# A Winograd-multiplied graph attention on one core: the last two block sums on VectorE, W_v's differences in another order, one counting pass later, attention paced anew

## The chip, the core and the metric

The kernel runs on one core of a Trainium2 chip. The metric is the device time of one execution in microseconds. The core's engines run side by side, each through its own list of instructions in order: TensorE (PE in the profile, PEld for its weight loads) multiplies, VectorE (DVE) and ScalarE (ACT) work on tiles in on-chip memory, GpSimd (POOL) does the same and also issues the gathers and scatters by index, and SyncE (SP) issues plain DMA transfers. An instruction waits at the head of its engine's list until the semaphores that it needs have come; what stands behind it on that engine waits too.

## The reference

```python
h = jnp.maximum(_layernorm(x, axis=-1), 0.0)
...
q = sent_embed @ W_q.T + b_q
k = sent_embed @ W_k.T + b_k
v = sent_embed @ W_v.T + b_v
scale = 1.0 / math.sqrt(sent_embed.shape[-1])
z = scale * (q @ k.T)
spare_z = z * adj_tensor
spare_z = jnp.where(spare_z == 0.0, jnp.asarray(-10000.0, spare_z.dtype), spare_z)
attn = jax.nn.softmax(spare_z, axis=1)
out = attn @ v
return jax.nn.relu(out)
...
x = x + _L0_gnn_ref(h, adj, ...)
```

x is 2708 x 1024, adj is 2708 x 2708 with about four ones in a row, the weights are 1024 x 1024, and everything is in float32. Since adj is so thin, the kernel never forms q @ k.T. It finds the edges of each row, gathers the few rows of h that they name, and takes scores and weighted sums of those alone.

## The kernel before

**Stages.** First the product of the two weights W_q and W_k is formed (called M, in four blocks; about the first 105 us), while the rows of x are normalised to h and written to `h_dram`, and while adj is searched. A tile is 128 rows. The search of tile k has two halves: `found` (steps f, i) takes the places of the ones with VectorE, and `counted` (step p) sums the row with one pass of ScalarE over the whole tile of adj (line 368). Both read the same buffer of three; whichever of them comes first in the program issues the load (`loaded`, line 360, on SP). Then rows are sorted by their number of edges, in two halves, and all later work goes by sorted tiles of 128 rows.

**Units.** The main loop (line 1225 on) runs over 20 units of two tiles each. Units 0 to 9 are q units: rows of h times M, which gives the q rows. Units 10 to 19 are o units: the attention's weighted sums u times W_v, which gives the output. Each unit is one Winograd product of a 2 x 2 block matrix: seven block products instead of eight. In the order of PE's list, for unit n, they are:

- second: s2·T1 into bank Y (line 1010, `psy<-wlow,s`)
- third: a12·M10 into bank X (`ps<-M,a`)
- fourth: s4·M11 into bank Z (`ps<-M,s`)
- fifth: s3·T2 into bank Y (`psy<-wlow,s`)
- then the first two of the next unit, `opened(n+1)`: a11·M00 into its X (`ps<-M,a`) and s1·T0 into its Z (`ps<-wlow,s`)
- seventh: a22·T3 into bank Y (`psy<-wlow,a`)

Each is four matmuls of 128x512 in float32, which the trace shows as eight records. T0 to T3 are four differences of the blocks of M, kept in `wlow`. When the q units are over, M's place takes the four blocks b11, b12, b21, b22 of W_v, loaded one by one during units 8 and 9 (line 1259), and VectorE forms T0 to T3 anew at line 1263: T0 = b12 - b11, T1 = b22 - T0, T2 = b22 - b12, T3 = b21 - T1. Each may be written only when unit 9 has used the old one.

**What surrounds the products.** `blocks` (line 711) prepares a unit's operands. The rows are either turned by PE (line 415, `pt<-ident,qr`, four groups of transposes in a unit) and copied by ScalarE (line 718), or, in units 10 to 14 (the "faced" tiles), loaded in quarters (line 700) and turned by VectorE (line 705). Then s1 and s3 are sums of two blocks on VectorE, and s2 and s4 are sums on the engine named in the call at line 1281, GpSimd for nearly all units (line 722, function `put`). `multiply` (line 1044) calls `after(0)` to `after(6)` between the products. The results leave the banks by ScalarE copies (line 1023: Y starts as a copy of X; line 1026: p5 from Z; line 1054: u2 from Y after the second product; lines 1088, 1099 in q units, 1118, 1134 in o units) and by two additions on VectorE: c12 (line 1094, or 1125 in o units) takes Z, c22 (line 1091, or 1121) takes Y after the fifth product. In o units ScalarE first copies Y for c22 (line 1075), in units 6 to 9 VectorE reads Y itself, and the seventh product, which goes on in Y, must wait for that reader.

**The attention** is a stream of steps on VectorE: `scores` (line 863, a product with a running sum over 128x1024), `weights` (small operations at lines 893 to 911 and, on ScalarE, line 872 or 898 and the start of the weighted sum at line 912 or 903) and `sums` (line 923). The gathered rows lie in 11 slots, 13 once M's place is free; a slot is filled by a gather on GpSimd (line 610) when its reader is done. Every call of `after` draws `share` microseconds of estimated steps from the stream (`advance`, line 999), so `share` fixes how many attention steps stand in VectorE's list between two steps of a unit. VectorE's list is in the order in which the program is written; the lists of PE, SP and, for the later units, of ScalarE and GpSimd are ordered by a scheduler that works with its own estimates.

**The steps table.** The search and the normalisation are written by hand into the units: `steps_at[(n, i)]` names what `follow` does in `after(i)` of unit n.

Of the kernel before, what the change touches and what calls it, by code (L numbers as in the profile page):

```python
# [65 lines left out]
def tile_preln_masked_attention(  # L66
# [12 lines left out]
    nc = tc.nc  # L79
# [353 lines left out]
    T = wlow.rearrange("p (k a) (b w) -> p k (a b) w", a=2, b=2)  # L433
# [180 lines left out]
    rows_of = {}  # L614
    FIRST = EARLY // 2
# [95 lines left out]
    def blocks(xa, xb, eng=None):  # L711


        ops = {}

        def held(name, bank):
            ops[name] = small(name).rearrange("p (c q) -> p c q", q=P)
            nc.scalar.copy(ops[name], bank)

        def put(name, a, b, op, eng=None):  # L720
            ops[name] = small(name).rearrange("p (c q) -> p c q", q=P)
            step = (eng or nc.vector).tensor_tensor(ops[name], a, b, op=op)  # L722
            if eng is None:
                behind.append(step)

        def faced_half(name, xt, s):
            ops[name] = small(name).rearrange("p (c q) -> p c q", q=P)
            faces(ops[name], xt, s * 4, s * 4 + 4)

        def upper():  # L730
            for s, name in enumerate(("a11", "a12")):
                if is_faced(xa):
                    faced_half(name, xa, s)
                else:
                    held(name, half_turned(xa, s))

        def lower():
            if is_faced(xb):
                faced_half("a22", xb, 1)
                faced_half("s3", xb, 0)  # L740
                put("s1", ops["a22"], ops["s3"], ALU.add)
                behind.append(nc.vector.tensor_sub(ops["s3"], ops["a11"], ops["s3"]))
            else:
                held("a22", half_turned(xb, 1))
                a21 = half_turned(xb, 0)
                put("s1", ops["a22"], a21, ALU.add)
                put("s3", ops["a11"], a21, ALU.subtract)
            put("s2", ops["s1"], ops["a11"], ALU.subtract, eng)
            put("s4", ops["a12"], ops["s2"], ALU.subtract, eng)

        return ops, upper, lower
# [11 lines left out]
    def natural_rows(n):  # L763
# [3 lines left out]
    ops_of = {0: blocks(*rows_of.pop(0))}  # L767
# [14 lines left out]
    steps_at = {(0, 0): "s4-5 p8 e9 +19 +20 +21", (0, 1): "r4 +0 +1 +2 i10.0-1", (0, 3): "p10", (0, 4): "i10.2-3 a4",  # L782
# [4 lines left out]
    steps_ahead = {(1, 5): "o1", (3, 6): "o0"}  # L787

# [199 lines left out]
    faced_tiles, whole_second = set(), []  # L988
# [236 lines left out]
    for n, unit in enumerate(units):  # L1225
        kind, ta, tb = unit
        now[:] = n, 0
        if n == FIRST:
            ordered.close()
            ordered.enter_context(tc.manual_schedule(engines={mybir.EngineType.DVE}))  # L1230
            nc.sync.dma_start(bp_dram, bp_sb[0:1, :])
        turn = n in (0, FIRST - 1)
        share = (20.0 if kind == "q" else 19.8) / 7
        nxt = units[n + 1] if n + 1 < len(units) else None
        if nxt is not None and nxt[0] == "o":
            share -= 1.3 / 7 * len(set(nxt[1:]) & faced_tiles)
        results = (q_results if kind == "q" else o_results)(ta, tb)

        def after(i):
            now[1] = i  # L1240
            if (n, i) in steps_ahead:
                follow(steps_ahead[n, i])
            if (n, i) == (2, 5):
                owe(8)
                owe(9)
                rows_of[FIRST] = load_rows(units[FIRST])
                owe(10)
                owe(6)
                owe(7)
                rows_of[FIRST + 1] = load_rows(units[FIRST + 1])  # L1250
                pooled.close()
            if (n, i) == (FIRST, 1):
                for g in slots[:HIGH - 3]:
                    nc.vector.memset(g, 0.0)
            b11, b12, b21, b22 = M[:, 0, 0], M[:, 0, 1], M[:, 1, 0], M[:, 1, 1]
            for at, place, src in (((-1, 0), b12, of_wv(0, 1)), ((0, 0), b11, of_wv(0, 0)), ((0, 2), T[:, 1], of_wv(1, 1)),
                                   ((0, 3), b21, of_wv(1, 0)), ((0, 4), b22, of_wv(1, 1))):
                if (n - last_q, i) == at:
                    nc.sync.dma_start(place, src)
            for at, place, a, b in (((0, 2), T[:, 0], b12, b11), ((0, 5), T[:, 1], T[:, 1], T[:, 0]),  # L1260
                                    ((1, 0), T[:, 3], b21, T[:, 1]), ((1, 1), T[:, 2], b22, b12)):
                if (n - last_q, i) == at:
                    nc.vector.tensor_sub(place, a, b)  # L1263
            if (n - last_q, i) == (1, 1):
                free.extend(M.rearrange("p i j (a c) w -> p i j a (c w)", a=2)[:, 0, 1, a, :] for a in range(2))
            if (n, i) == (FIRST, 5):
                next(stream)
            if (n, i) == (FIRST, 6):
                chain.append(behind[-1])
                next(stream)  # L1270
                nc.vector.tensor_tensor(bad, bad, total, op=ALU.not_equal)
            if (n, i) == (FIRST + 1, 6):
                marked(EARLY, NT)
            if (n, i) == (FIRST + 2, 4):
                nc.vector.tensor_scalar(msq, msq, MLIMIT, None, op0=ALU.is_gt)
            if n > FIRST + 1 or n == FIRST + 1 and i > 1:
                advance(share)
            if nxt is not None:

                if i == (3 if n == 0 else 4 if turn else 0):  # L1280
                    ops_of[n + 1] = blocks(*rows_of[n + 1], nc.gpsimd if n + 1 != FIRST - 1 else None)
                    with tc.issue_after(products[-1].ins) if n + 1 == FIRST else nullcontext():
                        ops_of[n + 1][1]()
                if i == (4 if n == 0 else 5 if turn else 2):
                    ops_of[n + 1][2]()
                    rows_of.pop(n + 1)
                    if n == last_q - 1:
                        all_rows()
                if i == 3:
                    banks_of[n + 1] = banks_for(bp_sb)  # L1290
                if i == 6 and n + 2 < FIRST:
                    natural_rows(n + 2)
                if i == (2 if n in (FIRST, last_q) else 4) and n + 2 > FIRST and n + 2 < len(units) and n + 2 not in rows_of:
                    while units[n + 2][0] == "o" and not done.issuperset(units[n + 2][1:]):
                        advance(1.0)
                    rows_of[n + 2] = load_rows(units[n + 2])
            if (n, i) in steps_at:
                follow(steps_at[n, i])
            if (n, i) == (3, 4):
                searched()  # L1300
            if (n, i) == (3, 5):
                for s in range(8, HIGH):
                    for c in range(0, D, D // 4):
                        clear = nc.gpsimd.memset(slots[s][:, c:c + D // 4], 0.0)
                        tc.add_manual_dep(clear.ins, counted_at[-1].ins.name,
                                          mybir.DependencyInfo(mybir.DependencyClass.Sync, mybir.DependencyReason.DATA),
                                          reason="not beside the counts")
            if i == 3 and units[n - 1][0] == "o" and NT - 2 in units[n - 1][1:]:
                tail(NT - 1)
            if nxt is None and i == 1:  # L1310
                while alone not in done:
                    advance(1.0)
                r, = load_rows(("o", alone))
                single["turned"] = turned(r, "alone")
            if nxt is None and i == 3:
                single["banks"] = banks_for(bp_sb)
            if n == last_q - 1 and i == 4:

                nc.sync.dma_start(bp_sb, bv.to_broadcast([P, D]))
            if (n, i) == (last_q, 1):  # L1320
                nc.vector.tensor_sub(bp_sb[:, NB:], bp_sb[:, NB:], bp_sb[:, :NB])

        multiply(n, results, after)
# [54 lines left out]
    with tc.If(some > 0):  # L1378
# [19 lines left out]
        with tc.tile_pool(name="big", bufs=1, side="right") as big, tc.tile_pool(  # L1398
# [34 lines left out]
            with tc.For_i(0, NT) as i:  # L1433
# [9 lines left out]
                q = gen.tile([P, D + 1], FT, tag="q", name="g_q")  # L1443
# [111 lines left out]
```

## Time and profile before

| | |
|---|---|
| median of 3 runs | 646.67 us (646.43 to 647.45) |
| the profiled execution | 648.94 us |
| its span, first to last instruction | 647.2 us |
| mean granted TensorE clock | 0.995 |
| DMA | 176.97 MB, 273 GB/s over the span |

The span is 1.7 us shorter than the profiled execution's own time; the rest lies before the first and behind the last instruction. In a row of the profile, `out<-in` are the program's tile names without numbers, the figure behind the engine's name is the line of the kernel, and a bracket at the end of a timeline's row says how long the engine sat idle just before it and what ended that. The timeline's first two columns are the start and the length in microseconds, and equal rows that follow each other are merged (their count stands behind the x). Rows with PEq, SPq or ACTq are the sequencer of that engine, as it issues a transfer.

### The profile page before, as it was taken

The page shows a single profiled execution, that of the slowest core. Times are in us where ns is not written, and L with a number is a line of the kernel's source. Part 1 is how long each engine was busy: PE and PEld are TensorE (multiplying, and loading weights), DVE is VectorE, ACT ScalarE, POOL GpSimd, SP SyncE. Part 2 cuts the span into 40 slices and gives each one's busy share as a digit, 9 for nine tenths or more (in the row PEclk, how much of TensorE's full clock was granted, in tenths as well). Part 3 has the DMA queues.
Part 4 walks back from the last instruction along what each step waited for, and adds up shares of the span by engine and source line. Part 5 has one row for each costly group of instructions (what it writes and reads, how often), then busy time and mean ns, then how long its engine had stood idle before and what let it go on. Part 6 is the DMA issues. An engine that isn't in the chain of part 4 may idle for free.

```text
span 647.2 us, 6198 instructions
## 1 busy us (share of the span) xinstructions
PE 628.8 (97%) x1651; PEld 317.6 (49%) x1651; DVE 529.4 (82%) x984; ACT 281.2 (43%) x423; POOL 412.8 (64%) x415
## 2 busy tenths in 40 slices
PE   9999999999989999999999989999989999999994
PEld 5777766444434544444444434444444444444441
DVE  5999789897897515987988999999999898898521
ACT  3548984958496523434421234352242233332300
POOL 2649950966857778674862666668868778763421
PEclk9999999999999999999999999999999999999998
DMA  8999997598796649887599988999999998972541
GB/s 340 407 354 317 361 347 279 190 361 294 243 300 226 230 125 318 283 307 213 172 291 368 275 329 242 335 298 321 346 370 313 329 259 257 274 238 65 142 166 54
DMA packets 60193, 176.97 MB, mean 273 GB/s; under 512 B 9799, under 2 KB 15255, under 8 KB 59512
## 3 DMA queue, kind: packets, MB, share of 16 engines
q0 software_dynamic: 25136, 78.41, 39.4%
q1 hardware_dynamic: 29514, 78.61, 34.6%
q10 hardware_dynamic: 5502, 19.48, 7.8%
q8 instruction: 15, 0.25, 0.2%
q14 instruction: 26, 0.21, 0.1%
HBM read 145.65 MB, written 40.74 MB: 288 GB/s over the span
## 4 chain that ended last, share of the span: by engine, by line
PE 57%; DVE 17%; issue 10%; DMA 7%; POOL 5%; ACT 2%; SPq 1%; POOLq 0%; DVEq 0%; ACTq 0%
PE ps L1010 22%; PE psy L1010 16%; PE ps_y L476 6%; DVE junk L863 6%; DVE u L923 5%; PE ps_x L476 4%; PE ps_z L476 4%; DMA g<-h_dram,tab 3%; PE pt L415 3%; DMA M<-in_wv_dram 2%; POOL g L610 2%; DMA adj<-in_adj_dram 1%; POOL y L1109 1%; POOL s L722 1%; DVE a L705 1%
## 5 line engine op out<-in xcount | busy, mean ns | idle before, releaser
L1010 PE MATMUL psy<-wlow,s 128*128 128x512 f32 x320 | 144.3, 594 | 5.8 <-DVE wlow L1263 1.9
L610 POOL DMA_INDIRECT g<-h_dram,tab x94 | 119.0, 1266 | 47.3 <-issue 18.6
L1010 PE MATMUL ps<-M,a 128*128 128x512 f32 x320 | 144.0, 593 | 0.0
L863 DVE SCALAR_TENSOR_TENSOR junk<-g,pq 128x1024 uint8<-128x1024 f32 x93 | 119.3, 1282 | 17.2 <-DMA g<-h_dram,tab 13.8
L923 DVE SCALAR_TENSOR_TENSOR u<-g,coef,u 128x1024 f32<-128x1024 f32 x70 | 100.6, 1438 | 5.1 <-ACT u L912 3.6
L1010 PEld LDWEIGHTS psy<-wlow,s 128*128 128x128 f32 x320 | 59.1, 190 | 76.6 <-issue 67.5
L1010 PEld LDWEIGHTS ps<-M,a 128*128 128x128 f32 x320 | 59.7, 190 | 70.4 <-issue 69.2
L1010 PE MATMUL psy<-wlow,a 128*128 128x512 f32 x160 | 72.1, 593 | 2.6 <-ACT taken L1075 2.2
L389 DVE FIND_INDEX8 at<-ones,adj 128x8 uint32<-128x685 f32 (+1 forms) x88 | 74.5, 865 | 0.0
L1010 PE MATMUL ps<-M,s 128*128 128x512 f32 x160 | 71.9, 592 | 0.0
L1010 PE MATMUL ps<-wlow,s 128*128 128x512 f32 x160 | 71.9, 592 | 0.0
L368 ACT ACTIVATE sized<-adj 128x2708 uint8<-128x2708 f32 (+1 forms) x22 | 54.2, 2466 | 7.0 <-DMA adj<-in_adj_dram 5.7
L298 POOL TENSOR_TENSOR hsum<-hsum,x 128x256 f32<-128x256 f32 (+1 forms) x56 | 38.7, 730 | 27.8 <-DVE wlow L444 21.8
L1010 PEld LDWEIGHTS psy<-wlow,a 128*128 128x128 f32 x160 | 30.2, 190 | 41.6 <-issue 37.3
L1010 PEld LDWEIGHTS ps<-wlow,s 128*128 128x128 f32 x160 | 30.3, 190 | 38.3 <-issue 36.8
L1010 PEld LDWEIGHTS ps<-M,s 128*128 128x128 f32 x160 | 30.3, 190 | 38.1 <-issue 37.8
L1109 POOL DMA_INDIRECT y<-in_x_dram,tab x19 | 33.5, 1765 | 18.8 <-ACT y L1126 8.0
L808 POOL DMA_INDIRECT out_dram<-y,tab x21 | 29.2, 1391 | 20.1 <-DVE flag L1346 7.5
L912 ACT ACTIVATE u<-g,coef 128x1024 f32<-128x1024 f32 x17 | 19.5, 1149 | 45.9 <-DVE coef L911 39.8
L722 POOL TENSOR_TENSOR s<-s,a 128x512 f32<-128x512 f32 x18 | 24.2, 1343 | 14.3 <-DVE s L722 14.1
L722 DVE TENSOR_TENSOR s<-a,pt 128x512 f32<-128x512 f32 x30 | 19.2, 682 | 16.7 <-ACT junk_m L375 5.6
L722 POOL TENSOR_TENSOR s<-a,s 128x512 f32<-128x512 f32 x18 | 30.1, 1674 | 1.3
(251 smaller groups left out, 884.0 us busy)
## 6 DMA issues: line engine op xcount, KB each, us to landing
adj<-in_adj_dram SPq DMA_DIRECT2D x21, 1354.0 KB
x<-in_x_dram SPq DMA_DIRECT2D x21, 512.0 KB
h_dram<-x ACTq DMA_DIRECT2D x21, 512.0 KB
q_late<-q SPq DMA_DIRECT2D x12, 512.0 KB
pq<-q_late SPq DMA_DIRECT2D x12, 512.0 KB
u_dram<-v ACTq DMA_DIRECT2D x10, 512.0 KB
or<-u_dram SPq DMA_DIRECT2D x40, 128.0 KB
M<-in_wv_dram SPq DMA_DIRECT2D x4, 1024.0 KB
```

The lines of the kernel that those rows point to most:

```text
L298: small.append(nc.gpsimd.tensor_add(hsum[:n, cols], hsum[:n, cols], xt[:n, cols]))
L368: nc.scalar.activation(sized[:n], a[:n, :, :PW], AF.Abs, accum_out=total[:n, t:t + 1])
L389: nc.vector.max_index(at[:n, k - first_k, g, :], ones[:n, 0:8], a[:n, g, :])
L476: mm = nc.tensor.matmul(bank, a_tile(o + H * a[0], a[1], i), b(o), start=first and o == 0, stop=(o == H - 1), skip_group_check=True)
L610: return nc.gpsimd.indirect_dma_start(out=dst, out_offset=None, in_=src, in_offset=off, bounds_check=N - 1, oob_is_err=False)
L722: step = (eng or nc.vector).tensor_tensor(ops[name], a, b, op=op)
L808: to = nc.gpsimd.indirect_dma_start(out=out, out_offset=bass.IndirectOffsetOnAxis(ap=ptab.bitcast(U32)[:n, t, SLOTS:SLOTS + 1], axis=0), i ...
L863: chained(lambda: nc.vector.scalar_tensor_tensor(junk, g_of[t][s], 1.0, tq[t], op0=ALU.mult, op1=ALU.mult, accum_out=zall[:, t, s:s + 1]))
L912: nc.scalar.activation(u, g_of[t][0], AF.Copy, scale=coef[:, 0:1])
L923: chained(lambda: nc.vector.scalar_tensor_tensor(u, g_of[t][s], coef[:, s:s + 1], u, op0=ALU.mult, op1=ALU.add))
L1010: mm = nc.tensor.matmul(bank, a[:, c, :], b[:, c, :], start=False, stop=(c == 3), skip_group_check=True)
L1109: return nc.gpsimd.indirect_dma_start(out=y[:n], out_offset=None, in_=x, in_offset=off, compute_op=ALU.add)
```

## The change

Four things change. The sums s2 and s4 of units 3 to 19 go to VectorE, behind s1 and s3 in its list; those of units 1 and 2 stay on GpSimd. T1 is formed at step (9, 4) instead of (9, 5), and T2 and T3 change places, so that T2 comes at (10, 0) and T3 at (10, 1). The counting pass p19 moves from `after(5)` to `after(6)` of unit 2, which is behind `opened(3)` and unit 2's last result in ScalarE's list. And `share` becomes 20.9/7 for all units (it was 20.0/7 in q units and 19.8/7 in o units), with 2.3/7 instead of 1.3/7 taken off for each faced tile of the next unit.

```diff
-                (2, 2): "p16", (2, 3): "p17 a8 k8 z", (2, 4): "p18", (2, 5): "f18 f19 p19", (2, 6): "f20 p20",
+                (2, 2): "p16", (2, 3): "p17 a8 k8 z", (2, 4): "p18", (2, 5): "f18 f19", (2, 6): "p19 f20 p20",
...
-        share = (20.0 if kind == "q" else 19.8) / 7
+        share = 20.9 / 7
         nxt = units[n + 1] if n + 1 < len(units) else None
         if nxt is not None and nxt[0] == "o":
-            share -= 1.3 / 7 * len(set(nxt[1:]) & faced_tiles)
+            share -= 2.3 / 7 * len(set(nxt[1:]) & faced_tiles)
...
-            for at, place, a, b in (((0, 2), T[:, 0], b12, b11), ((0, 5), T[:, 1], T[:, 1], T[:, 0]),
-                                    ((1, 0), T[:, 3], b21, T[:, 1]), ((1, 1), T[:, 2], b22, b12)):
+            for at, place, a, b in (((0, 2), T[:, 0], b12, b11), ((0, 4), T[:, 1], T[:, 1], T[:, 0]),
+                                    ((1, 0), T[:, 2], b22, b12), ((1, 1), T[:, 3], b21, T[:, 1])):
                 if (n - last_q, i) == at:
                     nc.vector.tensor_sub(place, a, b)
...
-                    ops_of[n + 1] = blocks(*rows_of[n + 1], nc.gpsimd if n + 1 != FIRST - 1 else None)
+                    ops_of[n + 1] = blocks(*rows_of[n + 1], nc.gpsimd if n + 1 < FIRST - 1 else None)
```

In the loop `n - last_q` is the unit's number less 9, and FIRST is 4.

## The prediction

> **What bounds the kernel now.** I read the page's first lines, then the waits of TensorE, then the timeline around each wait, on every engine.
>
> ```profile
> span 647.2 us, 6198 instructions
> PE 628.8 (97%) x1651; PEld 317.6 (49%) x1651; DVE 529.4 (82%) x984; ACT 281.2 (43%) x423; POOL 412.8 (64%) x415
> ...
> PE psy L1010 <- ACT taken L1075: 2.2, 1, 2.2
> PE psy L1010 <- DVE wlow L1263: 1.9, 1, 1.9
> PE psy L1010 <- ACT u L1054: 1.9, 1, 1.9
> PE psy L1010 <- ACT psy L1023: 1.8, 1, 1.8
> ...
> PE psy L1010 <- DVE q L1091: 0.4, 1, 0.4
> ```
>
> The first two rows are the page's, the others TensorE's waits in the main loop: engine, tile and line, releaser, total, times, longest. TensorE is busy for 97% of the span. None of the products' work is touched, so the change can only win these five waits, 2.2 + 1.9 + 1.9 + 1.8 + 0.4 = 8.2 us, and can lose without limit. The forecast is therefore a tally of five known waits and of those that may come in their place.
>
> ```profile
> 448.60:476.00 27.40, 25.20 (x65) 11.37 (x64) 26.39 (x44) 9.88 (x18) 20.26 (x15) 1.00 1.05 339
> ```
>
> This row gives one stretch of the late o units: its length, then the busy times of PE, PEld, DVE, ACT and POOL, the granted clock, the DMA share and the rate. VectorE is idle for only 27.40 - 26.39 = 1.01 us of 27.40, so the sums go to an engine with little room there.
>
> **p19, the 1.8 at unit 3.** The next rows are from the timeline and, fourth, from the DMA view of 197.9 to 201.1 us.
>
> ```profile
> 189.41 2.46 ACT L368 ACTIVATE sized<-adj 128x2708 uint8<-128x2708 f32 x1
> 191.87 0.58 ACT L1023 COPY psy<-ps 128x512 f32<-128x512 f32 x1
> 192.50 3.70 PE L1010 MATMUL psy<-wlow,s 128*128 128x512 f32 x8 [1.80 <-ACT psy L1023]
> ...
> 197.97 1.07 POOL L612 DMA_INDIRECT qr<-h_dram,tab  x1 [7.50 <-DMA h_dram<-x]
> ...
> q0 software_dynamic: 65, 0.27, 36.0%
> ...
> 202.57 0.14 PEld L415 LDWEIGHTS pt<-ident,qr 128*128 128x128 f32 x1 [0.34 <-issue]
> ```
>
> p19's pass holds ScalarE from 189.41 to 191.87 while TensorE wants the copy behind it. With p19 in `after(6)` the copy stands ahead and the 1.80 goes. The load of adj is still issued at the same place, by f19, so no transfer moves. But the next thing late is known: the transposes at 202.57 need rows gathered at 197.97, whose release is the landing of `h_dram<-x`, which the change doesn't move. By 201.1 only 0.27 MB in 65 packets of that queue had moved; TensorE, 1.8 earlier, would be there at about 200.8 and wait for the same landing. I give back 1.7 and keep 0.1, between 0 (nothing lands earlier) and 1.8 (all of it does, since the rows were seen used, not seen landing).
>
> **The order of W_v's differences.** The timeline once more, VectorE, then GpSimd and TensorE:
>
> ```profile
> 356.67 1.22 DVE L863 SCALAR_TENSOR_TENSOR junk<-g,pq 128x1024 uint8<-128x1024 f32 x1
> ...
> 358.95 0.71 DVE L705 STREAM_TRANSPOSE a<-or 128x512 f32<-128x512 f32 x1
> ...
> 360.35 0.69 DVE L722 TENSOR_TENSOR s<-a,s 128x512 f32<-128x512 f32 x1
> ...
> 361.69 4.88 DVE L923 SCALAR_TENSOR_TENSOR u<-g,coef,u 128x1024 f32<-128x1024 f32 x2
> 366.50 0.68 DVE L1094 TENSOR_TENSOR q<-ps,u 128x512 f32<-128x512 f32 x1
> 367.10 2.59 DVE L923 SCALAR_TENSOR_TENSOR u<-g,coef,u 128x1024 f32<-128x1024 f32 x2
> 369.61 0.68 DVE L1091 TENSOR_TENSOR q<-psy,p 128x512 f32<-128x512 f32 x1
> 370.20 2.28 DVE L1263 TENSOR_TENSOR wlow<-wlow 128x2048 f32<-128x2048 f32 x1
> 372.40 3.92 DVE L923 SCALAR_TENSOR_TENSOR u<-g,coef,u 128x1024 f32<-128x1024 f32 x3
> ...
> 379.76 1.22 DVE L863 SCALAR_TENSOR_TENSOR junk<-g,pq 128x1024 uint8<-128x1024 f32 x1
> 380.92 0.14 DVE L894 TENSOR_SCALAR coef<-keys 128x1 f32<-128x1 f32 x1
> ...
> 382.62 1.30 DVE L705 STREAM_TRANSPOSE a<-or 128x512 f32<-128x512 f32 x2
> 383.84 2.25 DVE L1263 TENSOR_TENSOR wlow<-M 128x2048 f32<-128x2048 f32 x1
> ...
> 392.16 0.69 DVE L722 TENSOR_TENSOR s<-a,s 128x512 f32<-128x512 f32 x1
> ```
>
> ```profile
> 362.00 1.27 POOL L722 TENSOR_TENSOR s<-s,a 128x512 f32<-128x512 f32 x1
> 363.35 2.14 POOL L722 TENSOR_TENSOR s<-a,s 128x512 f32<-128x512 f32 x1
> ```
>
> ```profile
> 370.34 3.70 PE L1010 MATMUL psy<-wlow,a 128*128 128x512 f32 x8 [0.43 <-DVE q L1091]
> ...
> 386.23 3.67 PE L1010 MATMUL psy<-wlow,s 128*128 128x512 f32 x8 [1.89 <-DVE wlow L1263]
> ```
>
> T2 at 383.84 ends 386.09 and TensorE waits for it from 386.23 - 1.89 = 384.34. In the changed program T1 (2.20 from start to start), two sums of line 923 (2.51), T3 (2.20) and two transposes (1.22) no longer stand between c22 and T2: T2 starts 8.1 earlier, near 376, and ends 6 before its use. The 1.89 goes. T3 comes after a score, a sum and the transposes, ending near 384, and its product is the last of the seven, two products later than that: no wait.
>
> T1 pays for it: it now precedes c22 (line 1091), and behind c22 waits the seventh product. From T0's end to c22: out go a score and a weights step (356.67 to 358.95, 2.28); in come one L923 (2.51 / 2 = 1.25), T1 (2.20) and two sums (360.35 to 361.69, 1.34); and L923 runs without its neighbours on GpSimd, at 2.51 the pair and not 366.50 - 361.69 = 4.81, 2.30 less. Sum: -2.28 + 1.25 + 2.20 + 1.34 - 2.30 = +0.21. With TensorE 0.1 earlier the 0.43 becomes 0.7. Bounds: 0 where a sum is cheaper, 2.7 where GpSimd's neighbours had cost nothing.
>
> T1's load, issued by SP, moves behind the first quarter of the next unit's load by line 700.
>
> ```profile
> 342.71 11.65 DMA M<-in_wv_dram
> 352.78 0.33 SPq L1259 DMA_DIRECT2D wlow<-in_wv_dram  x1
> ```
>
> From the chain of waits, a block took 11.65 from issue to landing; 352.78 plus 0.6 for the quarter's issue plus 11.65 is 365.0, and VectorE comes to T1 at about 356.7 + 1.25 + 1.34 + 1.34 + 1.25 + 2.51 + 0.6 = 365.0 (the two 1.34 are transposes and sums). No wait, with no room to spare; rival D.
>
> In unit 11, s1 (392.16) follows c22 by T1 and two L923 less (2.20 + 2.51), one weights step and one score more (1.70 + 1.16): 1.85 earlier, plus 0.21, so it ends near 391.2. TensorE reaches its product two products (7 us) after 384.34, about 391.4. Gathered rows awaited on the way could hold it: 0 to 1.9, and I take 0.4.
>
> **The sums on VectorE.** In units 6 to 19 the group rows (count, total, mean ns, idle before) are:
>
> ```profile
> L923 DVE SCALAR_TENSOR_TENSOR u<-g,coef,u 128x1024 f32<-128x1024 f32 x70 | 100.6, 1438 | 5.1 <-ACT u L912 3.6
> ...
> L722 POOL TENSOR_TENSOR s<-a,s 128x512 f32<-128x512 f32 x14 | 25.0, 1784 | 0.9
> L722 POOL TENSOR_TENSOR s<-s,a 128x512 f32<-128x512 f32 x14 | 19.1, 1362 | 14.3 <-DVE s L722 14.1
> ```
>
> VectorE gains 14 x 2 sums; at 1.34 the pair that is 18.8 us. GpSimd loses 44.1 that lay beside other work. What VectorE gets back is bounded: below by L923 alone, (1.438 - 1.295) x 70 = 10.0; above by 14 pairs at 2.30, 32.2. I take 24, above the middle, as other operations (scores, transposes) meet the pairs too. Net -5 us for VectorE, between -13.4 and +8.8. The row at 361.69 against that at 367.10 is the ground for it.
> The Trainium skill's page "SBUF — State Buffer", section "Who interferes with whom", says that a VectorE instruction with two inputs in SBUF contends with a GpSimd instruction that reads SBUF; the trace's 4.88 against 2.59 agrees, and by it, too, the sums would be relieved.
>
> **The two late waits.** Both stand behind the attention's `L912` in ScalarE's list:
>
> ```profile
> 467.32 0.69 DVE L1125 TENSOR_TENSOR u<-ps,u 128x512 f32<-128x512 f32 x1
> 469.93 1.15 ACT L912 ACTIVATE u<-g,coef 128x1024 f32<-128x1024 f32 x1 [1.26 <-DVE coef L911]
> ...
> 564.94 1.15 ACT L912 ACTIVATE u<-g,coef 128x1024 f32<-128x1024 f32 x1 [3.69 <-DVE coef L911]
> ```
>
> In unit 13, L912 waits for VectorE and holds L1075 behind it (the 2.2). The changed program has L1075 ahead of it. What then holds L1075 is the copy of line 1126, released by line 1125 at 467.32, or 469.93 - 467.32 = 2.6 before L912 begins; what is missing VectorE makes good, being 5 us better over 14 units: gone. In unit 17 the order stays, L912 holds L1054 (the 1.9), and TensorE by then is some 3.5 earlier itself, so VectorE must be 1.9 + 3.5 = 5.4 earlier; with about 5 I leave 0.5 of the 1.9 (0 to 1.9). The new `share` places as many attention steps ahead of unit 17 as the old one; where it differs (units 8 to 10) it is in the sums above.
>
> **Sum.** Won: 0.1 (p19), 1.9 (T2), 2.2 (unit 13), 1.4 (unit 17); lost: 0.3 (c22), 0.4 (s1). Net 5.6 - 0.7 = 4.9. Against the profiled execution, 648.94 (span 647.2), that is 644.0. That execution lies 2.27 above the median, so the same 4.9 taken from 646.67 gives 641.8.
>
> **The rivals.**
> B, the gathers land earlier as well: TensorE's transposes wait less, 1.7 more is won, 640.1. For it: the gather of unit 4 shares its queues with transfers that may move. Against: its release is not moved.
> A, the late waits stay (something other than VectorE's list, such as a gathered row, sets L911): 2.2 + 1.4 lost again, 645.4. For it: DMA share 1.05 in the row of 448.60. Against: the waits are named VectorE's, whose idle there is 1.0.
> C, slower: VectorE becomes the bound. If the relief fails, 18.8 us come on top of an engine with 1.01 of 27.40 idle, 12.5 over 14 units of 24.4; 6.3 are left for TensorE to wait, 653.0. It decides from where the relief is under 6.3, and the lower bound, 10.0, is above. The Trainium skill's "Perfetto Trace Analysis", section "Optimizing Scalar/DVE Operations", holds that from a saturated VectorE some work may better go to GpSimd, the reverse of this change, and adds that their shared read port may spoil it; the trace's 4.81 against 2.51 speaks for the addition.
> D, slower: T1's load lands late. T1, c22 and the seventh product wait one for one; from a landing at 365.0 + 4.9 + 1.3 = 371.2 on the kernel is slower. I price it at 8 late: 641.8 + 8 - 0.7 = 649.1. For it: DMA is crowded there, with the 11.65 above. Against: the load is only 0.6 later than before.
> That the change doesn't do what it says falls away: in the built program the late sums do stand in VectorE's list, and only units 1 and 2 keep theirs on GpSimd.
>
> **How the numbers follow.** Chances: forecast 0.57, B 0.12, A 0.14, C 0.11, D 0.06. The forecast's own range is 640.2 (c22, s1 and unit 17 all at 0) to 644.7 (s1 and unit 17 at 1.9 each). The 8-in-10 range reaches down to 639.0 (B, and unit 17's 0.5 and s1's 0.4 gone too, 639.2) and up to 645.6, past A; C and D, 0.17, are left out. A measurement of this kernel can tell about 0.2%, 1.3 us, from no change: faster is below 645.4, slower above 648.0. A lies on the bound, half to each: faster 0.57 + 0.12 + 0.07 = 0.76, same 0.07, slower 0.17.
>
> **What would show it.** L1023 before unit 3's product in time, and L415 at 202.57 waiting 1.5 or more for the gather instead of 0.34: p19 and its give-back. The product at 386.23 with no wait, line 1091 near 369.8 with 0.7 before its product: the T order. L923's mean falling from 1438 to about 1300, VectorE's busy time up by less than 18.8 minus what L923 loses: the relief. No wait on L1075, and under 1 on L1054: the late units. Wrong would be waits on VectorE or ScalarE repeated in several late units (C), a wait of T1 for its load (D), or L923 as slow as before.

## The result and the profile after

Against the kernel before, the changed kernel takes a ratio of 0.9886, interval 0.9858 to 0.9915: a median of 640.60 us over 4 runs (639.94 to 641.38). The forecast was 641.8, between 639.0 and 645.6. The ratio is taken against four runs of before, of which one took 651.47; the median of 646.67 shown before gives 640.60 / 646.67 = 0.9906. In a second session, on a chip called C below, the same kernel came to 0.9915 (0.9880 to 0.9951). The two intervals overlap; the second stands beside the experiments below. Here are the page's first rows of the changed kernel and then all of TensorE's waits (engine, tile and line, releaser, total, times, longest):

```profile
span 638.1 us, 6156 instructions
PE 627.8 (98%) x1651; PEld 317.9 (50%) x1651; DVE 522.4 (82%) x1016; ACT 283.6 (44%) x423; POOL 360.2 (56%) x383
...
PE ps_y L511 <- POOL hsum L121: 1.2, 1, 1.2
PE ps L1010 <- DVE s L722: 0.4, 1, 0.4
```

The five waits of 8.2 us are gone; 0.4 for s1 of unit 11 is new, as forecast. With TensorE's busy time 1.0 less (628.8 to 627.8, at a mean granted clock of 0.997 instead of 0.995) that is 8.2 - 0.4 + 1.0 = 8.8 of the span's 9.1; a wait of 0.2 at line 1010 that no engine had released is gone too. The median fell by 6.1, from the 646.67 shown before, where 4.9 were forecast. The first profile of before, at 648.94, was itself 2.3 above its median, so part of the 9.1 belongs to that one execution. The first experiment shows which waits do.

VectorE has 32 instructions more, two sums for each of the 16 units 4 to 19 (those of unit 3 stood on VectorE before as well), and is busy for 7.0 us less, 529.4 to 522.4. Line 923 gives the largest part, in the group rows from 240 us on (count, total, mean ns, idle before):

```profile
L923 DVE SCALAR_TENSOR_TENSOR u<-g,coef,u 128x1024 f32<-128x1024 f32 x69 | 88.4, 1281 | 7.0 <-ACT u L912 5.8
...
L722 DVE TENSOR_TENSOR s<-a,s 128x512 f32<-128x512 f32 x19 | 13.2, 692 | 1.0
```

The mean fell from 1438 to 1281 ns, as forecast (about 1300), and the sums are there at 0.69 each. Last, the stretch of W_v's differences, from the timeline: T0 of before, which the prediction doesn't show, and then the changed kernel.

```profile
354.46 2.29 DVE L1263 TENSOR_TENSOR wlow<-M 128x2048 f32<-128x2048 f32 x1 [1.79 <-DMA M<-in_wv_dram]
```

```profile
351.76 2.28 DVE L1263 TENSOR_TENSOR wlow<-M 128x2048 f32<-128x2048 f32 x1
...
362.34 2.28 DVE L1263 TENSOR_TENSOR wlow<-wlow 128x2048 f32<-128x2048 f32 x1
364.54 2.60 DVE L923 SCALAR_TENSOR_TENSOR u<-g,coef,u 128x1024 f32<-128x1024 f32 x2
367.06 0.68 DVE L1091 TENSOR_TENSOR q<-psy,p 128x512 f32<-128x512 f32 x1
...
373.34 2.28 DVE L1263 TENSOR_TENSOR wlow<-M 128x2048 f32<-128x2048 f32 x1
```

```profile
367.80 3.70 PE L1010 MATMUL psy<-wlow,a 128*128 128x512 f32 x8
...
381.63 3.60 PE L1010 MATMUL psy<-wlow,s 128*128 128x512 f32 x8
...
389.03 3.67 PE L1010 MATMUL ps<-wlow,s 128*128 128x512 f32 x8 [0.36 <-DVE s L722]
```

From the start of T0 to c22 it is 367.06 - 351.76 = 15.30 us, against 369.61 - 354.46 = 15.15 before: 0.15 more where 0.21 was forecast. T2 now starts 8.3 before its use. But T0 began 2.7 us earlier than before, where VectorE had sat idle ahead of it for 1.79 us, and TensorE came to its product only 369.91 - 367.80 = 2.1 earlier, and so c22 came in time. The forecast of a 0.7 us wait had held T0's place fixed. The experiments show how much it moves.

### The profile page after: what moved, and what is told of

Same layout as the page of the kernel before. It is cut to its first block, busy times and chain, and to the rows that moved or that the text cites. A ratio compares the mean times of both kernels' runs of the same rounds, so it can differ in the third digit from the quotient of the medians.

```text
span 638.1 us, 6156 instructions
## 1 busy us (share of the span) xinstructions
PE 627.8 (98%) x1651; PEld 317.9 (50%) x1651; DVE 522.4 (82%) x1016; ACT 283.6 (44%) x423; POOL 360.2 (56%) x383
## 4 chain that ended last, share of the span: by engine, by line
PE 90%; issue 4%; POOL 2%; DMA 2%; DVE 1%; POOLq 0%; ACT 0%; ACTq 0%; DVEq 0%
PE ps L1010 40%; PE psy L1010 29%; PE ps_y L476 6%; PE ps_x L476 4%; PE ps_z L476 4%; PE pt L415 4%; POOL g L610 2%; DMA v_dram<-u 1%; DMA M<-h_dram,tab 1%; PE ps_y L511 1%; DVE junk L863 0%; PE ps_h L1218 0%; PE ps_v L594 0%; DVE u L923 0%; DVE s L722 0%
## 5 line engine op out<-in xcount | busy, mean ns | idle before, releaser
L863 DVE SCALAR_TENSOR_TENSOR junk<-g,pq 128x1024 uint8<-128x1024 f32 x93 | 113.8, 1224 | 13.4 <-DMA g<-h_dram,tab 10.4
L923 DVE SCALAR_TENSOR_TENSOR u<-g,coef,u 128x1024 f32<-128x1024 f32 x69 | 88.4, 1281 | 7.0 <-ACT u L912 5.8
L808 POOL DMA_INDIRECT out_dram<-y,tab x21 | 27.4, 1306 | 32.0 <-DMA y<-in_x_dram,tab 15.8
L912 ACT ACTIVATE u<-g,coef 128x1024 f32<-128x1024 f32 x18 | 20.7, 1149 | 35.8 <-DVE coef L911 35.6
L276 ACT ACTIVATE x<-x,r 128x1024 f32<-128x1024 f32 (+1 forms) x22 | 25.9, 1232 | 6.6 <-POOL r L266 6.6
L476 PE MATMUL ps_y<-wlow 128*128 128x512 f32 x64 | 27.6, 592 | 0.0
```

Of the source, the lines that this page charges most:

```text
L276: nc.scalar.activation(xs[i][:n], xs[i][:n], AF.Relu, bias=r[:n, 4, i:i + 1], scale=r[:n, 3, i:i + 1])
L476: mm = nc.tensor.matmul(bank, a_tile(o + H * a[0], a[1], i), b(o), start=first and o == 0, stop=(o == H - 1), skip_group_check=True)
L808: to = nc.gpsimd.indirect_dma_start(out=out, out_offset=bass.IndirectOffsetOnAxis(ap=ptab.bitcast(U32)[:n, t, SLOTS:SLOTS + 1], axis=0), i ...
L863: chained(lambda: nc.vector.scalar_tensor_tensor(junk, g_of[t][s], 1.0, tq[t], op0=ALU.mult, op1=ALU.mult, accum_out=zall[:, t, s:s + 1]))
L923: chained(lambda: nc.vector.scalar_tensor_tensor(u, g_of[t][s], coef[:, s:s + 1], u, op0=ALU.mult, op1=ALU.add))
```

## The experiments

Four edits make up the change: p19's place, the order of W_v's differences, the sums, and the share. Each was made alone and each was taken out of the whole. The first four experiments ran on one chip (A), the next four on another (B), the last four on a third (C); every ratio is to the kernel of before on the same chip, whose medians were 647.65, 652.02 and 652.22 us. On which chip the first two profiles, of before and of the changed kernel, were taken is not on record.

**Before, once more** (chip A), no edit.

> The kernel of before, unchanged, for a second profile of it. In the first profile ScalarE sat idle for 2.97 us before line 1054 of unit 2 with a releaser that the profile cannot name, and two more such waits follow in units 2 and 5. Theory: the 1.8 us wait of TensorE for line 1023 at unit 3 belongs to the program; it is there again, about 1.8, and the time is 1.000 of before. Rival: it was that execution's own; the new profile has no nameless wait, no wait for line 1023 (or under 0.5), and its span is some 2 us under 647.2.

Measured 1.0002 (0.9976 to 1.0027). Two of the five waits are left in its profile; the others in its list are 1.2 or less, and at line 1010 only one of 0.2:

```profile
PE psy L1010 <- ACT taken L1075: 2.2, 1, 2.2
...
PE psy L1010 <- DVE wlow L1263: 0.8, 1, 0.8
```

The rival holds. There is no wait for line 1023, none for line 1054 in unit 17 and none for line 1091; T2's is 0.8 instead of 1.9. The first profile differs in the row below, ScalarE in unit 2, against the same instruction in this second profile behind it:

```profile
172.44 0.59 ACT L1054 COPY u<-psy 128x512 f32<-128x512 f32 x1 [2.97 <-remote]
```

```profile
169.25 0.60 ACT L1054 COPY u<-psy 128x512 f32<-128x512 f32 x1
```

It is the same program, and it waits for the same product there. In the one execution ScalarE starts 3.2 us later, and the profile knows no releaser ("remote"; called a nameless wait below). What stands behind it on ScalarE was late too: the copy of line 1023 (191.87 against 187.89), and with it the 1.8 us at unit 3, but also the stores of h. So the 1.8 came from this lateness together with p19.

**p19 alone** (chip A).

```diff
-  (2, 5): "f18 f19 p19", (2, 6): "f20 p20",
+  (2, 5): "f18 f19", (2, 6): "p19 f20 p20",
```

> Before with p19 alone moved. Theory (p19's pass holds the copy of line 1023): TensorE's 1.8 at unit 3 is gone and the time falls by 0.1 (the gather of unit 4 takes it back) to 1.8 us. Rival (the wait was that of one late execution): 0.0 within the measurement. Every later wait of TensorE (T2's 1.9, L1075's 2.2, L1054's 1.9) stays as it was in both.

Measured 1.0010 (0.9992 to 1.0028): nothing, as the rival has it. Waits for T2 (1.9), L1054 (1.7) and L1075 (1.0) are all still there.

**The order alone** (chip A).

```diff
-  ((0, 5), T[:, 1], T[:, 1], T[:, 0]), ((1, 0), T[:, 3], b21, T[:, 1]), ((1, 1), T[:, 2], b22, b12)
+  ((0, 4), T[:, 1], T[:, 1], T[:, 0]), ((1, 0), T[:, 2], b22, b12), ((1, 1), T[:, 3], b21, T[:, 1])
```

> Before with the order of W_v's differences alone changed. Theory: TensorE's 1.9 for T2 is gone; line 1091 comes about 1.2 later (T1 2.2 ahead of it, other steps 1.0 less), so its 0.4 becomes some 1.6 to 2.6; net -0.7 us at best and +0.3 at worst. Rival (T2's wait is only moved on to s1 of unit 11 or to the late units): 0.0 to +1.

Measured 1.0077 (1.0054 to 1.0101): 5.0 us slower, worse than either had it. TensorE's waits in the main loop, and VectorE's T0 and c22:

```profile
PE psy L1010 <- DVE q L1091: 3.3, 1, 3.3
PE ps L1010 <- DVE s L722: 2.2, 1, 2.2
PE ps L1010 <- ACT ps L760: 2.1, 1, 2.1
...
PE psy L1010 <- ACT taken L1075: 1.2, 1, 1.2
```

```profile
354.46 2.29 DVE L1263 TENSOR_TENSOR wlow<-M 128x2048 f32<-128x2048 f32 x1 [2.45 <-DMA M<-in_wv_dram]
...
371.79 0.68 DVE L1091 TENSOR_TENSOR q<-psy,p 128x512 f32<-128x512 f32 x1
```

T2's wait is gone, and in its place stand 3.3 for c22 and 2.2 for s1 of unit 11. From T0 to c22 it is 17.33 us, 2.18 more than the 15.15 of before: T1's 2.20 from start to start.

**The sums alone** (chip A).

```diff
-  ops_of[n + 1] = blocks(*rows_of[n + 1], nc.gpsimd if n + 1 != FIRST - 1 else None)
+  ops_of[n + 1] = blocks(*rows_of[n + 1], nc.gpsimd if n + 1 < FIRST - 1 else None)
```

> Before with the late sums alone on VectorE. Theory (the two engines hold each other up): line 923's mean falls from 1438 ns to about 1280, VectorE's busy time falls, TensorE's waits for L1075 and L1054 go (2.2 + 1.9), T2's 1.9 stays or shrinks; 3 to 5 us faster. Rival (no relief, VectorE pays 18.8 us): L923 stays near 1438, TensorE waits repeatedly for VectorE, up to 6 us slower.

Measured 0.9964 (0.9946 to 0.9982): 2.3 us, below the theory's 3 to 5 but on its side. VectorE is relieved in full: L923 at 1281 ns, busy for 522.5 us. T0 and c22:

```profile
350.88 2.29 DVE L1263 TENSOR_TENSOR wlow<-M 128x2048 f32<-128x2048 f32 x1 [0.51 <-DMA M<-in_wv_dram]
365.06 0.68 DVE L1091 TENSOR_TENSOR q<-psy,p 128x512 f32<-128x512 f32 x1
```

14.18 us, 0.97 less than before. T2's wait shrank to 0.4, and none is left for L1054. What the theory had wrong is the other late wait. First TensorE's, then VectorE and ScalarE ahead of it:

```profile
PE psy L1010 <- ACT taken L1075: 3.1, 1, 3.1
```

```profile
490.43 1.22 DVE L863 SCALAR_TENSOR_TENSOR junk<-g,pq 128x1024 uint8<-128x1024 f32 x1 [2.89 <-DMA g<-h_dram,tab]
...
491.58 0.69 DVE L1125 TENSOR_TENSOR u<-ps,u 128x512 f32<-128x512 f32 x1
```

```profile
492.30 0.63 ACT L1126 ACTIVATE y<-u 128x512 f32<-128x512 f32 x1 [0.40 <-DVE u L1125]
```

L1075 follows at 492.84 and still costs 3.1, now in unit 14, and no L912 holds it. Line 1126 stands ahead of it and waits for line 1125 of VectorE, which stands behind a score that waited 2.89 us for its gathered row. So relief alone doesn't remove the late waits: here VectorE ran into a gather.

**The whole without the sums** (chip B).

```diff
-  nc.gpsimd if n + 1 < FIRST - 1 else None
+  nc.gpsimd if n + 1 != FIRST - 1 else None
```

> The changed kernel with the late sums back on GpSimd. Theory (the engines hold each other up, and the other edits need the time that VectorE gets back): L923 again near 1438 ns, T1 ahead of line 1091 brings TensorE's wait there to 2 to 3.5 us as in the run with the order alone, s1 of unit 11 some 2 late; 1.003 to 1.010 of before. Rival (the gain is the new pace's): under 0.995.

Measured 0.9979 (0.9952 to 1.0007), between the two. L923 is back at 1414 ns, and TensorE waits 3.7 for line 1091, about as the theory has it. It does not wait for s1 of unit 11, which the theory had, nor for anything in the late units.

**The whole without the order** (chip B).

```diff
-  ((0, 4), T[:, 1], T[:, 1], T[:, 0]), ((1, 0), T[:, 2], b22, b12), ((1, 1), T[:, 3], b21, T[:, 1])
+  ((0, 5), T[:, 1], T[:, 1], T[:, 0]), ((1, 0), T[:, 3], b21, T[:, 1]), ((1, 1), T[:, 2], b22, b12)
```

> The changed kernel with W_v's differences in the old order. Theory (the order removes one wait for T2, which is 0.4 to 1.9 us in the runs so far, and costs nothing once VectorE is relieved): T2's wait is back at 0.4 to 2, 0.989 to 0.992 of before. Rival (the order is worth nothing beside the other edits): as the changed kernel, 0.9886, with no wait at line 1263.

Measured 0.9923 (0.9900 to 0.9945). T2's 1.9 is back, and beside it stand 1.7 for c22 of unit 9 and 0.8 for s1 of unit 11. By its time the order is worth nothing that can be told: the run without p19's move, on the same chip, came to 0.9920 with it.

**The whole without the share** (chip B).

```diff
-  share = 20.9 / 7
+  share = (20.0 if kind == "q" else 19.8) / 7
...
-  share -= 2.3 / 7 * len(set(nxt[1:]) & faced_tiles)
+  share -= 1.3 / 7 * len(set(nxt[1:]) & faced_tiles)
```

> The changed kernel with the old share. Theory (the pace decides in which late unit ScalarE's L1075 or L1054 stands behind a late L912; with the sums alone one wait of 3.1 us for L1075 is left in unit 14): one such wait of 2 to 3.5 us is back, 0.991 to 0.995 of before. Rival (the pace changes nothing, as the prediction had it): 0.9886, no such wait.

Measured 1.0016 (0.9993 to 1.0039): with the old share the other three edits win nothing at all. That is more than the theory asked for, and it refutes the prediction, which gave the share nothing beyond the steps that it moves past c22 and s1. TensorE's waits (the profiled execution ran at a granted clock of 0.982, so they are read for their kind more than for their size):

```profile
PE psy L1010 <- DVE q L1091: 3.1, 1, 3.1
PE pt L415 <- DMA qr<-h_dram,tab: 2.6, 1, 2.6
PE psy L1010 <- ACT taken L1075: 2.5, 1, 2.5
PE ps L1010 <- DVE s L722: 2.2, 1, 2.2
...
PE psy L1010 <- ACT u L1054: 0.5, 1, 0.5
```

L1075 and L1054 in the late units are here again. L1075 waits as with the sums alone, behind a score that waited (3.38 us) for its gathered row. T0 and c22, of VectorE:

```profile
359.11 2.29 DVE L1263 TENSOR_TENSOR wlow<-M 128x2048 f32<-128x2048 f32 x1 [2.10 <-DMA M<-in_wv_dram]
...
375.50 0.68 DVE L1091 TENSOR_TENSOR q<-psy,p 128x512 f32<-128x512 f32 x1
```

That is 16.39 us. VectorE's own rows are not longer in this execution: line 923 stands at 1281 ns.

**The whole without p19's move** (chip B).

```diff
-  (2, 5): "f18 f19", (2, 6): "p19 f20 p20",
+  (2, 5): "f18 f19 p19", (2, 6): "f20 p20",
```

> The changed kernel with p19 where it was. Theory now, after the second profile of before: the wait at unit 3 was that of one execution, so the move brings nothing: as the changed kernel, 0.9886 within 0.25%. Rival (with the rest of the change p19 does hold line 1023): a wait of up to 1.8 us for line 1023, 0.991.

Measured 0.9920 (0.9890 to 0.9949), 0.05% from the whole's ratio on chip C. The rival's wait is there, 1.1 us for line 1023, and yet nothing is lost. The next profile shows why.

**The whole, once more** (chip C), no edit.

> The changed kernel once more, on one chip with the three beside it. Theory (a chip differs in the nameless waits of units 2 to 5, which make VectorE late, and the change's gain partly hangs on them): between 0.987 and 0.992 of before; where nameless waits are in its profile, TensorE waits for line 1091 by up to 3 us, where none are, by 0. Rival (the gain is the program's): 0.9886 whatever the profile shows.

Measured 0.9915 (0.9880 to 0.9951). ScalarE has the nameless wait before line 1054 (3.88 us) and the waits are

```profile
PE pt L415 <- DMA qr<-h_dram,tab: 2.2, 1, 2.2
PE psy L1010 <- DVE q L1091: 2.2, 1, 2.2
```

```profile
197.12 1.07 POOL L612 DMA_INDIRECT qr<-h_dram,tab  x1 [7.29 <-DMA h_dram<-x]
...
203.11 1.06 PE L415 MATMUL pt<-ident,qr 128*128 128x128 f32 x8 [2.21 <-DMA qr<-h_dram,tab]
```

Here is the give-back of the prediction. With a late ScalarE and p19 moved, line 1023 is in time and TensorE then waits for the gather, whose release (197.12, against 197.97 in the first profile of before) has hardly moved. In the changed kernel's first profile the same gather went out at 192.12, since the stores of h were not late. Either way p19's move brings next to nothing: with a late ScalarE another wait takes the place of its own, and without one there is no wait. For c22 the rows are

```profile
356.31 2.29 DVE L1263 TENSOR_TENSOR wlow<-M 128x2048 f32<-128x2048 f32 x1
...
371.61 0.68 DVE L1091 TENSOR_TENSOR q<-psy,p 128x512 f32<-128x512 f32 x1
...
372.35 5.40 PE L1010 MATMUL psy<-wlow,a 128*128 128x512 f32 x8 [2.20 <-DVE q L1091]
```

From T0 it is 15.30 us again, to the hundredth, but TensorE is ready for its product at 372.35 - 2.20 = 370.15. The theory fits: 2.2 where nameless waits are, 0 where none are. These are two profiles of the changed kernel, and how the nameless waits of units 2 to 5 come to make c22 late in unit 9 was not followed.

**The share alone** (chip C).

```diff
-  share = (20.0 if kind == "q" else 19.8) / 7
+  share = 20.9 / 7
...
-  share -= 1.3 / 7 * len(set(nxt[1:]) & faced_tiles)
+  share -= 2.3 / 7 * len(set(nxt[1:]) & faced_tiles)
```

> Before with the new share alone. Theory now (without the new share the other three edits together come to 1.0016, so it carries most of the gain: VectorE comes earlier to c22, s1 and the late units' steps): 0.993 to 0.997, and fewer of TensorE's waits for L1263, L1075 and L1054. Rival (as predicted, the new share only pays for the sums on VectorE and the later T2): 0.999 to 1.003 by itself.

Measured 0.9975 (0.9950 to 1.0000): 1.6 us by its middle, between the two sides, the interval touching none. L1075 and L1054 are gone from the list, L1263 (1.6), L1091 (2.6) and s1 (1.9) are not. ScalarE has nameless waits here, and with p19 in its old place line 1023 is waited for again (1.9).

**The whole with only the faced part of the share** (chip C).

```diff
-  share = 20.9 / 7
+  share = (20.0 if kind == "q" else 19.8) / 7
```

> The changed kernel with the old share (20.0 and 19.8) but the new 2.3 taken off for each faced tile. Theory (what counts is that in units 9 to 13 fewer attention steps stand ahead of the sums, of T1 and of c22): within 0.3% of the changed kernel beside it, TensorE's wait for line 1091 under 1. Rival (what counts is the larger share of the q units, which brings the attention forward before unit 9): near the kernel with the old share, 0.999 to 1.003.

Measured 0.9964 (0.9935 to 0.9992), half way between the whole beside it and the whole without the share on chip B; neither side holds alone. TensorE's waits, and then T0 and c22:

```profile
PE psy L1010 <- DVE q L1091: 5.6, 1, 5.6
PE pt L415 <- DMA qr<-h_dram,tab: 2.3, 1, 2.3
```

```profile
359.18 2.29 DVE L1263 TENSOR_TENSOR wlow<-M 128x2048 f32<-128x2048 f32 x1 [4.38 <-DMA M<-in_wv_dram]
...
376.43 0.68 DVE L1091 TENSOR_TENSOR q<-psy,p 128x512 f32<-128x512 f32 x1
```

Against the whole without the share, s1's wait and the late ones are gone with the 2.3 for faced tiles; for s1 it may also be that TensorE waits 2.5 longer at c22. Against the whole, c22's wait is 5.6 instead of 2.2, and the rows say why. VectorE comes to T0 early, sits idle for 4.38 us until W_v's block has landed, and then needs 17.25 us to c22. In the whole, two scores and a weights step that here stand behind T0 are done ahead of it, two steps of line 923 come in their place, T0 waits for nothing, and it is 15.30 to c22. So the 20.9 gives VectorE attention steps to do in time in which it would sit idle.

**The sums twice** (chip C): the whole, where GpSimd also forms both differences of each late unit in pieces, into a small bf16 tile that nobody reads.

```diff
+            if eng is None:
+                for a, b in ((ops["s1"], ops["a11"]), (ops["a12"], ops["s2"])):
+                    for c in range(8):
+                        idle = work.tile([P, 64], BF, tag="idle", name="idle", bufs=1)
+                        cols = slice(c % 2 * 64, c % 2 * 64 + 64)
+                        nc.gpsimd.tensor_tensor(idle, a[:, c // 2, cols], b[:, c // 2, cols], op=ALU.subtract)
```

> The changed kernel with GpSimd doing both sums a second time, in 16 pieces of 128x64 whose result nobody reads. No product and no other engine waits for them, only the buffers are held. Theory (it is the reading of GpSimd that slows VectorE): line 923's mean goes back up from 1281 ns by 50 to 160, VectorE's busy time by 8 to 25 us, and 2 to 6 us of the gain are lost. Rival (it was the waiting for GpSimd's results): L923 stays at 1281 and the time within 0.2% of the changed kernel beside it.

Measured 1.1218 (1.1177 to 1.1259), and by neither's mechanism. The groups of VectorE and GpSimd (lines behind the edit are six higher, so 869 is 863 and 929 is 923):

```profile
L869 DVE SCALAR_TENSOR_TENSOR junk<-g,pq 128x1024 uint8<-128x1024 f32 x93 | 115.3, 1240 | 89.1 <-DMA g<-h_dram,tab 86.9 <-issue 0.6
L929 DVE SCALAR_TENSOR_TENSOR u<-g,coef,u 128x1024 f32<-128x1024 f32 x69 | 89.3, 1294 | 6.6 <-ACT u L918 5.4
```

```profile
L755 POOL TENSOR_TENSOR idle<-a,s 128x64 bf16<-128x64 f32 x144 | 102.8, 714 | 10.8
L755 POOL TENSOR_TENSOR idle<-s,a 128x64 bf16<-128x64 f32 x144 | 94.6, 657 | 27.2 <-DVE s L722 17.4
```

The pieces take GpSimd 197 us, its gathers come late, and VectorE's scores wait 86.9 us for them. Yet line 923 stays at 1294 ns, although 57 of all its 84 executions at 128x1024 overlap with a piece (1298 ns in the mean). By its time the experiment doesn't tell the theories apart. Its trace does more. GpSimd, and then VectorE:

```profile
588.83 0.33 POOL L755 TENSOR_TENSOR idle<-s,a 128x64 bf16<-128x64 f32 x1
...
590.34 1.23 POOL L755 TENSOR_TENSOR idle<-s,a 128x64 bf16<-128x64 f32 x1
```

```profile
590.17 1.23 DVE L869 SCALAR_TENSOR_TENSOR junk<-g,pq 128x1024 uint8<-128x1024 f32 x1 [1.64 <-DMA g<-h_dram,tab]
```

A piece with nothing beside it takes 0.33 us. One that begins during a score takes 1.23 and ends 591.57 - 591.40 = 0.17 behind it. In this trace 109 of the 288 pieces end 0.16 to 0.18 us behind the end of a score or of line 923 with which they overlap. So the two engines do hold each other up here as well, but it is GpSimd that waits.

In the kernel of before it was VectorE. Counted in its first profile, 16 of the 84 executions of line 923 at 128x1024 overlap with a sum of GpSimd and take 2155 ns in the mean; the other 68 take 1281, as all 84 do in the changed kernel, where none overlaps. The longer mean is thus wholly that of the instructions that run beside GpSimd's sums, and not a wait for their results. That it is the reading which collides, and what decides which engine waits, was not shown.

## Why the prediction came out

The number held and so did most of the sums worked out from rows. What each edit is worth did not. On chip B, where the whole is represented by the run without p19's move (0.9920), taking out one edit costs:

| edit | forecast, us | alone (chips A and C) | taken out of the whole (chip B) |
|---|---|---|---|
| p19 | 0.1 won | 1.0010 | - |
| order | 1.9 - 0.3 - 0.4 = 1.2 won | 1.0077 | 0.9923 - 0.9920 = 0.0003, 0.2 us |
| sums, with the late waits | 3.6 won | 0.9964 | 0.9979 - 0.9920 = 0.0059, 3.8 us |
| share | 0, beside the 1.03 within c22's sum | 0.9975 | 1.0016 - 0.9920 = 0.0096, 6.3 us |

The differences are taken between middles. On chip B each ratio's interval is 0.2 to 0.3% to either side, and that of a difference some 0.4%, 2.6 us. The share's and the sums' differences are clear of zero; the order's 0.2 can't be told from the 1.2 that was forecast.

- **p19**: right, its give-back to the gather included, as the second run of the whole shows. The 1.8 itself, taken as the program's, belonged to executions with a late ScalarE. The profiles divide without exception, the doubled sums left aside. With nameless waits and p19 in its old place TensorE waits 1.1 to 1.9 for line 1023 (three profiles), with them and p19 moved 1.5 to 2.6 for the gather (five), and without them for neither (five). Rival B's earlier gather, at 192.0 to 193.3 instead of 197.1 to 198.3, stands in all five profiles without nameless waits, the second of before among them (192.04), and is no gain of the change.
- **From T0 to c22**: right term by term. The order adds 17.33 - 15.15 = 2.18 (forecast 2.20). The sums alone take off 0.97 (forecast 2.30 - 1.34 = 0.96), in the whole 0.56. The share takes off 375.50 - 359.11 - 15.30 = 1.09 in the step from the whole without it to the whole (forecast 2.28 - 1.25 = 1.03).
- **c22's wait**: this step failed. It was put at 0.7 because T0's start was held where one profile had it. T0 has two things to wait for, VectorE's list and the landing of W_v's block. With the old share of the q units VectorE sits idle ahead of T0 for that block in six of seven profiles (the doubled sums left aside), by 0.5 to 4.4 us; with 20.9 in one of six, by 0.3. TensorE is ready for the seventh product 369.91 - 354.46 = 15.45 us after T0's start in that profile, 367.80 - 351.76 = 16.0 in the changed kernel's first and 370.15 - 356.31 = 13.8 in its second. That spread is larger than the sum that was worked out, and the wait came to 0, 2.2 and (without p19's move) 3.0. That is where the order pays: it ends T2's wait in every run that has it, and brings c22 2.2 us later.
- **The sums' relief**: right. VectorE's net was put at -5 us, from -13.4 to +8.8, and is -7.0. Added up by line, line 923 gives back 14.0 us, the scores 5.4 and the small operations of the weights step (lines 894, 896, 906 and 911) 8.6; the sums cost 21.9. Beside line 923 the forecast had named the scores and the transposes; the small operations stand in the transposes' place. Every run with the 128x512 sums on GpSimd has line 923 at 1414 to 1438 ns, every run with them on VectorE alone at 1281 or 1282. That the two engines slow each other when they run at once is shown by the instructions that overlap, in the last experiment's trace and in that of before.
- **The late waits**: gone as forecast, in unit 13 by the step that was forecast and in unit 14 not. In the changed kernel's first profile L1075 of unit 13 stands ahead of L912 and is held by line 1126:

```profile
459.77 0.64 ACT L1126 ACTIVATE y<-u 128x512 f32<-128x512 f32 x1 [6.88 <-DVE u L1125]
460.31 0.56 ACT L1075 COPY taken<-psy 128x512 f32<-128x512 f32 x1
461.46 1.15 ACT L912 ACTIVATE u<-g,coef 128x1024 f32<-128x1024 f32 x1 [0.59 <-DVE coef L911]
```

The sums alone put it there too (457.51 against 464.39). The step "VectorE makes good, being 5 us better" failed one unit later: with the sums alone VectorE is 7 us better, meets a gathered row that has not landed, and L1075 waits 3.1. In units 10 to 19 a wait for L1075 or L1054 stands in the profiles of all five kernels with the old 1.3 per faced tile (before, p19, the order and the sums alone, the whole without the share) and, the doubled sums left aside, in none of the six with 2.3. TensorE's earlier waits, which give VectorE time, do not explain this: the order alone and the whole without the share have over 5 us of them in units 9 to 11 (3.3 + 2.2 and 3.1 + 2.2) and still a late wait, and the changed kernel's first profile has 0.4 and no late wait. So it is the faced part of the share that ends them, which one of the six has alone. How it does so was not followed; in the changed kernel VectorE waits for no gathered row ahead of line 1125 of unit 14.
- **The share**: the step that failed most. "The new share places as many attention steps ahead of unit 17 as the old one" counted steps at one place; for units 8 to 10 the prediction counted those that move past c22 (2.28 - 1.25 = 1.03) and s1, and for the rest it let unit 17 stand. It left out the idle time ahead of T0, which the 20.9 fills, and units 11 to 14, where two more sums and the faced tiles' transposes crowd together and the 2.3 takes attention steps out.
- **Rival A** (late waits stay, as something like a gathered row sets them) came true for the sums alone and for the whole without the share, **C** nowhere, **D** nowhere: T1 never waits for its load, in any of the runs.

The terms can't be added. Alone, the four ratios come to 1.0010 + 1.0077 + 0.9964 + 0.9975 - 4 = 0.0026, 1.7 us lost, where the whole wins 0.0085 on chip C: the order alone loses 5.0 us, and the share has to pay for it. Taken out one by one, the edits cost 10.3 us by their middles, where the whole, represented as above, wins 0.0080 x 652 = 5.2. The forecast was right in the list of waits that would end and in what VectorE would win; it was wrong in which edit ends which wait. That its sum came out is in part luck: three of the five waits in the tally were not in the second profile of the same program, the wait for c22 lies between 0 and 3.0 us where 0.7 was worked out, and the share, which carries the most, was all but left out of the sum. Its ratio, 641.8 / 646.67 = 0.9925, lies in the second run's interval and just above the first's.

## What to carry to other kernels

Where one profile's waits are to be counted as gains, take a second profile of the same program first: three of the five waits here were absent in it and a fourth was smaller. A step moved ahead on a crowded engine pays with its full length at whatever consumer it is put before, and whether that shows depends on how far that engine lags there, a number to be taken as a range over executions. When work is added to an engine whose list also carries a paced background stream, set the pace anew with it: here that was worth more than the move itself (6.3 against 3.8 us, each taken out of the whole). Whether two engines slow each other is best read from single instructions, those that overlap against those that don't, and on both engines, since it may be either that waits.

## What the runs showed of the hardware that was not expected

VectorE's instructions of 128x1024 and GpSimd's of 128x512 or 128x64 held each other up when they ran at once. Beside sums of 128x512 it was VectorE's line 923 that became longer (2155 instead of 1281 ns, 16 executions); beside pieces of 128x64 it was GpSimd's piece, which ended 0.16 to 0.18 us behind VectorE's instruction (109 of 288), while line 923 stayed at 1298.

On chips B and C, ScalarE or VectorE sat idle in units 2 to 5 for 0.8 to 11.6 us at a time with no releaser that the profile can name, in all eight profiles; on chip A in none of four. The kernel of before takes 652.0 and 652.2 us there, and 647.65 on A. They wait for a product or a transpose of TensorE. In the one followed above, line 1054 of unit 2, the product had ended 3.2 us before. What holds these instructions stays open.
